# Attention scores of a multi-query kernel: the queries of two heads as one stationary operand of 64 rows and 128 columns

## The chip, the cores and the metric

The kernel runs on one core of one Trainium2 chip. The metric is the device time of one execution in microseconds (us); the smaller is the better. A core has five engines that run side by side, each through its own instructions in their order, and that wait for each other by semaphores: TensorE (PE, matrix products; its weight loads are listed apart as PEld), VectorE (DVE), ScalarE (ACT), GpSimd (POOL) and SyncE (SP), which issues most of the transfers.

## The reference

A multi-query attention with one null key, causal and masked, over 64 sequences of 128 tokens with 512 features, 16 heads of 64 and one head of keys and values; all in float32.

```python
xn = layernorm(x, g_in)
q = (xn @ Wq).reshape(b, n, H, DH).transpose(0, 2, 1, 3) * scale   # H = 16, DH = 64
kv = xn @ Wkv
k, v = kv[..., :DH], kv[..., DH:]
# null key and value put ahead of k and v; null bias ahead of attn_bias
sim = jnp.einsum('bhid,bjd->bhij', q, k) + bias
sim = where(causal, neg, sim); sim = where(mask, sim, neg)
attn = softmax(sim)
out = jnp.einsum('bhij,bjd->bhid', attn, v) ... @ Wo
return x + layernorm(out, g_out)
```

The change is in the product `einsum('bhid,bjd->bhij', q, k)`, the scores.

## The kernel before, in words

The 64 sequences are taken in groups of four (`g`, 16 groups) for the projections of queries, keys and values, and in pairs (`d`, 32 pairs) for the attention. The program is in one fixed order, written out by hand: after a start-up, which holds the scores of pair 0, it calls `turn(d)` and `body(d)` or `body_full(d)` for the pairs up to 29, then `turn_end` and `body_end` for the last two, then `body_last`. The order of the calls is the order of the instructions on each engine. `turn(d)` holds the scores of the pair's two sequences, `a` and `b`, and the value products of the pair before; `body_full(d)` holds the exponentials of the pair and fills TensorE meanwhile with the query products of the next group (lines 603 and 697), the key and value products (line 404) and the output products (line 998) of the pair before.

The queries of a group lie in the tiles `qT[g, j, h]`, 128 partitions each. The partitions are two heads (`r`) of 64 features each; along the free axis come `f % 2`, the sequence, the half `hf` of the sequence's 128 queries, the half `u` of the heads, and 64 queries. So one head is given by `u` (2), `f` (4) and `r` (2). The keys lie in `kT`, held twice: on the partitions 0 to 63 and, copied there, on 64 to 127, since both `r` need the same keys.

`scores(b, hf, tiles)` (line 765) makes the scores of one sequence for half of its queries. For `hf = 0` these are the first 64 queries, which by causality need 64 keys (`nk = 64`); for `hf = 1` the last 64, with all 128 keys. The result stands in PSUM, in one room for each `r`, with the partitions (`u`, query) and the free axis (`f`, key): two heads above each other. In the loops over `f`, `r` and `u`, each product on line 780 contracts over 64 partitions (the rows of head `r`), has 64 stationary columns (the queries of one head) and 64 or 128 moving columns (the keys), and it writes 64 partitions, 0 to 63 or 64 to 127 by `u`. There are 16 such products for each sequence and half, 2,048 in the program. The rooms go by the tags of their PSUM pools (`sc_Y`, `sc_w`, `sc_a`, `sc_X`, `sc_c`, and `ps` for the room of two banks); the rooms of `r = 0` and of `r = 1` are always apart.

`scores_add` (DVE, line 795) then adds the scores onto bias and mask in SBUF, `scores_max` (DVE, line 802) takes the row maxima, `exps` (ACT, line 811) the exponentials with their sums, `rinv` and `scale` (DVE 829, POOL 833) divide, `blocks_T` (DVE, line 849) transposes, and `values` (TensorE, line 911) multiplies by the values, in products of 32 rows and 64 columns.

In `turn(d)` the order on TensorE is: scores of `a` and of `b` for `hf = 0`, scores of `a` for `hf = 1`, scores of `b` for `hf = 1`, then the value products of the pair before. So a pair has one block of scores, between the output products (line 998, 128 rows and 128 columns) and the value products.

Of the kernel before, what the change touches and what calls it, by code (L numbers as in the profile page):

```python
# [17 lines left out]
def kernel(  # L18
# [59 lines left out]
    nc = tc.nc  # L78
    B, N, DIM = x.shape
    H = attn_bias.shape[0]  # L80
    DH = w_kv.shape[1] // 2
# [8 lines left out]
    Q = 32  # L90
# [182 lines left out]
    xT, qT, vr = {}, {}, {}  # L273
# [117 lines left out]
    kT = hp.tile([P, NQ, GB, Q], FP, tag="kT", name="kT", bufs=1)  # L391
# [365 lines left out]
    def rooms(b, hf, tiles):  # L757

        nk = N if hf == 1 else NL
        return [  # L760
            pool.tile([P, NF, nk], FP, tag=tag, name=f"sc_{b}_{hf}_{tag}")
            for pool, tag in tiles
        ]

    def scores(b, hf, tiles=None):
        g, t = divmod(b, GB)
        nk = N if hf == 1 else NL
        if tiles is None:
            whole = ps_s.tile([P, 2, NF * nk], FP, tag="s", name=f"ps_{b}_{hf}")
            whole = whole.rearrange("p r (f j) -> p r f j", f=NF)  # L770
            home = [whole[:, r] for r in range(2)]
            pss[b, hf] = whole
        else:
            home = rooms(b, hf, tiles)
            pss[b, hf] = home
        for f in range(NF):
            for r in range(2):
                rows = slice(r * DH, (r + 1) * DH)
                for u in range(2):
                    nc.tensor.matmul(  # L780
                        home[r][u * DH : (u + 1) * DH, f, :],
                        qT[g, f // 2, t // 2][rows, f % 2, t % 2, hf, u],
                        kT[rows, 0 : nk // Q, t, :],
                        start=True,
                        stop=True,
                    )

    pss = {}

# [302 lines left out]
    def turn(d):  # L1092

        a, b, p = 2 * d, 2 * d + 1, 2 * d - 2
        g = d // 2 + 1
        homes = (ps_y, "Y"), (ps_q, "a")
        if d == 1:
            homes = homes[::-1]
        scores(a, 0, (homes[0], (ps_w, "w")))
        scores(b, 0, (homes[1], (ps_w, "w")))  # L1100
        scores(a, 1)
        scores(b, 1, ((ps_y, "X"), (ps_q, "c")))
        scores_add(a, 0)
        scores_add(b, 0)
        scores_max(a, 0)
        scores_add(a, 1)
        scores_add(b, 1)
        po = values_rooms(p)
        steady = 3 < d < PAIRS - 2
        values(p, WIDE if steady else ())  # L1110
        values(p + 1, (WIDE if d % 2 else WIDE[1:]) if steady else ())
        if d % 2 and (d + 1) // 2 < NG:
            mask_neg((d + 1) // 2)
        bias_add(a + 2)
        if d % 2 == 0:
            token_sum(g, 1)
            token_sum(g, 2)
        exps(a, 0)
        values_out(p, po)
# [715 lines left out]
```

## Time and profile before

| what | value |
|---|---|
| median of 3 runs | 1023.64 us (1023.05 to 1023.94) |
| the profiled execution, its own time | 1022.45 us |
| its span, first to last instruction | 1020.6 us |
| granted TensorE clock, mean | 1.000 |
| busy: TensorE products, weight loads | 1012.9 us, 902.0 us |
| busy: VectorE, ScalarE, GpSimd | 860.8, 672.8, 775.0 us |
| records of products on line 780 | 4,096, as many of weight loads |

The profile is of one execution. Its span is 1.85 us shorter than the time that this execution was given, and that time 1.2 us shorter than the median. "Busy" counts the union of the records of an engine; the ends of products on TensorE are modelled, so a record's start is firmer than its length. A form such as `64*64 64x128 f32` is a product of 64 rows and 64 stationary columns, whose moving operand has 64 partitions and 128 columns. A row of the waits tells who waited for whom, the total in us, how often, and the longest.

### The profile page before, as it was taken

The numbers are of one execution on the slowest core, as the hardware profiler recorded it, in microseconds if no ns is written. First come the engines' busy times: TensorE is split into PE (matmuls) and PEld (weight loads), VectorE is DVE, ScalarE is ACT, GpSimd is POOL, SyncE is SP. The second block draws the span as 40 slices with busy tenths as digits, with TensorE's granted clock in tenths as the row PEclk, the third lists the DMA queues.
The fourth block names the chain that finished last, engine by engine and source line by source line (L and its number), as shares of the span: only waits on it lengthen the run. The fifth ranks groups of instructions, "written<-read, shape, count | busy, mean of one in ns | idle before, by whom it ended". The sixth has DMA issues, their size and how long they took to land.

```text
span 1020.6 us, 31143 instructions
## 1 busy us (share of the span) xinstructions
PE 1012.9 (99%) x12285; PEld 902.0 (88%) x12285; DVE 860.8 (84%) x1849; ACT 672.8 (66%) x2675; POOL 775.0 (76%) x621
## 2 busy tenths in 40 slices
PE   9999999999999999999999999999999999999997
PEld 9888888888888888888888888888888888888886
DVE  6877778888888988889888888888888888878787
ACT  5766677656677565686666776566765667856583
POOL 4997779678696876959768596785968769587686
PEclk9999999999999999999999999999999999999999
DMA  7415243151431425224152341514314152141221
GB/s 219 139 31 151 67 117 112 31 163 65 143 99 61 120 67 152 88 76 124 51 161 76 105 121 35 164 63 138 102 49 136 64 152 89 71 103 33 68 85 62
DMA packets 73833, 100.84 MB, mean 99 GB/s; under 512 B 32212, under 2 KB 36056, under 8 KB 71896
## 3 DMA queue, kind: packets, MB, share of 16 engines
q1 hardware_dynamic: 73392, 98.47, 32.3%
q8 instruction: 96, 1.57, 0.6%
q14 instruction: 49, 0.40, 0.1%
q10 hardware_dynamic: 296, 0.40, 0.1%
HBM read 63.19 MB, written 33.55 MB: 95 GB/s over the span
## 4 chain that ended last, share of the span: by engine, by line
PE 95%; ACT 2%; POOL 1%; DVE 1%; issue 0%; DMA 0%; POOLq 0%; DVEq 0%
PE pyX L998 20%; PE pa L603 13%; PE pi L697 11%; PE pyY L998 10%; PE po L911 8%; PE pkv L404 6%; PE pyw L998 5%; PE pc L603 4%; PE ps L780 3%; PE pq L499 3%; PE pa L554 2%; PE sc_X L780 2%; PE sc_Y L780 2%; PE pc L697 2%; ACT s L811 2%; PE pc L554 1%
## 5 line engine op out<-in xcount | busy, mean ns | idle before, releaser
L811 ACT ACTIVATE s<-s,nmax 128x65 f32<-128x65 f32 (+1 forms) x1024 | 370.9, 366 | 62.2 <-DVE nmax L802 62.2
L833 POOL TENSOR_TENSOR s<-s,rinv 128x512 f32<-128x512 f32 (+1 forms) x132 | 189.7, 1448 | 115.4 <-DVE rinv L829 112.9
L745 POOL TENSOR_TENSOR s<-biasp,mneg 128x1552 f32<-128x1552 f32 (+1 forms) x65 | 206.2, 3175 | 30.7 <-DVE s L795 21.2
L811 ACT ACTIVATION_READ_ACCUMULATOR s<-s,nmax 128x1 f32 x1024 | 194.5, 190 | 0.0
L725 DVE TENSOR_TENSOR qT<-pi,qT 128x128 f32<-128x128 f32 (+1 forms) x376 | 123.6, 340 | 35.9 <-PE pi L697 28.8
L1034 ACT COPY y<-pyX 128x256 f32<-128x256 f32 x29 | 10.8, 373 | 180.7 <-PE pyX L998 180.7
L802 DVE TENSOR_REDUCE nmax<-s 128x8 f32<-128x1032 f32 (+1 forms) x128 | 121.6, 950 | 0.1
L849 DVE STREAM_TRANSPOSE sb<-s 128x1536 f32<-128x1536 f32 (+1 forms) x68 | 113.6, 1674 | 2.1 <-POOL s L833 1.7
L998 PE MATMUL pyX<-wT,oT 128*128 128x256 f32 x464 | 109.7, 379 | 0.0
L998 PE MATMUL pyX<-wo,oT 128*128 128x256 f32 x464 | 109.7, 379 | 0.0
L978 POOL TENSOR_TENSOR oT<-oT 128x512 f32<-128x512 f32 x64 | 81.1, 1278 | 26.4 <-PE pyw L998 24.1
L998 PEld LDWEIGHTS pyX<-wT,oT 128*128 128x128 f32 x464 | 84.0, 190 | 9.2
L998 PEld LDWEIGHTS pyX<-wo,oT 128*128 128x128 f32 x464 | 84.0, 190 | 9.2
L911 PE MATMUL po<-sb,vr 32*64 32x128 f32 (+1 forms) x3700 | 86.2, 315 | 0.1
L911 PEld LDWEIGHTS po<-sb,vr 32*64 32x64 f32 x3700 | 74.8, 131 | 9.5 <-issue 5.3
L930 ACT ACTIVATE oT<-po,nv 128x512 f32<-128x512 f32 (+1 forms) x127 | 73.9, 660 | 0.4 <-PE po L911 0.4
L404 PE MATMUL pkv<-xT,wkv 128*128 128x256 f32 x256 | 63.3, 391 | 0.0
L998 PE MATMUL pyw<-wo,oT 128*128 128x256 f32 x256 | 60.5, 379 | 0.0
L998 PE MATMUL pyY<-wo,oT 128*128 128x256 f32 x256 | 60.5, 379 | 0.0
L998 PE MATMUL pyY<-wT,yS 128*128 128x256 f32 x256 | 60.5, 379 | 0.0
L614 ACT COPY qT<-pa 128x512 f32<-128x512 f32 x78 | 45.4, 582 | 17.7 <-PE pa L603 17.7
L404 PEld LDWEIGHTS pkv<-xT,wkv 128*128 128x128 f32 x256 | 46.2, 189 | 10.0 <-issue 4.8
(231 smaller groups left out, 2510.1 us busy)
## 6 DMA issues: line engine op xcount, KB each, us to landing
res<-in_x_dram SPq DMA_DIRECT2D x64, 256.0 KB
out_dram<-y SPq DMA_DIRECT2D x63, 256.0 KB
x<-in_x_dram SPq DMA_DIRECT2D x62, 256.0 KB
xd<-xb SPq DMA_DIRECT2D x14, 1024.0 KB
xT<-xd SPq DMA_DIRECT2D x56, 256.0 KB
vr<-vd SPq DMA_DIRECT2D x64, 128.0 KB
kT<-kT SPq DMA_DIRECT2D x32, 64.0 KB
vd<-vb SPq DMA_DIRECT2D x32, 64.0 KB
```

What stands on the lines that cost most here:

```text
L404: nc.tensor.matmul(pkv, wkv[:, kc, :], xT[g][:, t : t + 2, kc, :], start=(kc == 0), stop=(kc == KC - 1),)
L603: nc.tensor.matmul(prod[tag][:, i], w[:, kc, f * P : (f + 1) * P], t[:, :, kc, :], start=first, stop=(kc == HK - 1), skip_group_check=not ...
L697: nc.tensor.matmul(to, inner_w[k][i][:, h], inner_x[k, g][i], start=(i == 1), stop=True, skip_group_check=(i != 1),)
L725: nc.vector.tensor_tensor(o, p, o, ALU.add)
L745: nc.gpsimd.tensor_tensor(S[b][:, :, keys], biasp[:, :, keys], mneg[:, t, keys] .unsqueeze(1) .broadcast_to([P, R8, keys.stop - keys.start ...
L802: nc.vector.tensor_reduce(nmax[b][:, hf], S[b][:, :, WITH_NULL[hf]], AX.X, ALU.max, negate=True)
L811: nc.scalar.activation(row, row, AF.Exp, bias=nmax[b][:, hf, k : k + 1], accum_out=rsum[b][:, hf, k : k + 1],)
L833: nc.gpsimd.tensor_tensor(sv, sv, rinvs[b, hf][:, lo:hi].unsqueeze(2).broadcast_to([P, hi - lo, sv.shape[2]]), ALU.mult,)
L849: nc.vector.transpose(sbs[b][:, :, lo:hi].rearrange("p j e q -> p e j q"), S[b][:, lo:hi, 1 : ROW - 1].rearrange("p e (j k) -> p e j k", k=Q),
L911: nc.tensor.matmul(po[s][rows, to : to + n], vr[g][quad, t, PLACE[j], :], sb[quad, slots, r * NF : (r + 1) * NF, :], start=(turn == 0), st ...
L978: eng.tensor_tensor(o, a, b, op)
L998: nc.tensor.matmul(prod[key], h[:, c, :], w[:, c, :], start=(start and c == 0), stop=(c == HC - 1), skip_group_check=not start,)
```

## The change

The loop over `u` goes. One product takes the queries of both heads `u` as one stationary operand of 64 rows and 128 columns, which lie side by side in `qT`, and writes all 128 partitions of the room. Rows, moving operand, rooms, and the order of `f` and `r` are the same.

```diff
         for f in range(NF):
             for r in range(2):
                 rows = slice(r * DH, (r + 1) * DH)
-                for u in range(2):
-                    nc.tensor.matmul(
-                        home[r][u * DH : (u + 1) * DH, f, :],
-                        qT[g, f // 2, t // 2][rows, f % 2, t % 2, hf, u],
-                        kT[rows, 0 : nk // Q, t, :],
-                        start=True,
-                        stop=True,
-                    )
+                nc.tensor.matmul(
+                    home[r][:, f, :],
+                    qT[g, f // 2, t // 2][rows, f % 2, t % 2, hf].rearrange(
+                        "p u i -> p (u i)"
+                    ),
+                    kT[rows, 0 : nk // Q, t, :],
+                    start=True,
+                    stop=True,
+                )
```

On TensorE, in a pair's turn, this is the place where the scores of `b` with 64 keys end (`sc_0_a` and `sc_0_w`, the rooms of `r = 0` and `r = 1`) and those of `a` with 128 keys follow (`ps_1`, both rooms), then the first of `b` with 128 keys (`sc_1_X`, `sc_1_c`). Each row gives the size of the result and, where there are several alike, their number. Before:

```order
L780 MATMUL sc_0_a<-kT,qT_1_0_1693 64x64 x2
L780 MATMUL sc_0_w<-kT,qT_1_0_1693 64x64 x2
L780 MATMUL ps_1_1959<-kT,qT_0_0_1308 64x128 x8
L780 MATMUL ps_1_1959<-kT,qT_1_0_1693 64x128 x8
L780 MATMUL sc_1_X<-kT,qT_0_0_1308 64x128 x2
L780 MATMUL sc_1_c<-kT,qT_0_0_1308 64x128 x2
```

And of the changed kernel, at the same place, where the product stands on line 779:

```order
L779 MATMUL sc_0_a<-kT,qT_1_0_1565 128x64
L779 MATMUL sc_0_w<-kT,qT_1_0_1565 128x64
L779 MATMUL ps_1_1815<-kT,qT_0_0_1212 128x128 x4
L779 MATMUL ps_1_1815<-kT,qT_1_0_1565 128x128 x4
L779 MATMUL sc_1_X<-kT,qT_0_0_1212 128x128
L779 MATMUL sc_1_c<-kT,qT_0_0_1212 128x128
```

Two products of 64 result partitions became one of 128, everywhere alike; nothing else stands in another place, on TensorE or on the other engines.

## The prediction

> **What bounds the kernel now.** I read the page's first and fourth parts, then TensorE's waits, then the instructions of the changed line 780, then the timeline of one steady pair.
>
> ```profile
> PE 1012.9 (99%) x12285; PEld 902.0 (88%) x12285; DVE 860.8 (84%) x1849; ACT 672.8 (66%) x2675; POOL 775.0 (76%) x621
> ...
> PE 95%; ACT 2%; POOL 1%; DVE 1%; issue 0%; DMA 0%; POOLq 0%; DVEq 0%
> ```
>
> A matmul engine at 99% need not be the limit, since its ends are modelled. Its waits settle it. The whole list for TensorE has two rows, 2.0 us in all:
>
> ```profile
> PE busy L1667 <- POOL neg L255: 1.4, 1, 1.4
> PE pyc L998 <- DVE y L1032: 0.6, 1, 0.6
> ```
>
> So TensorE is never held up by another engine between the start and the last pair, and its instructions run in a fixed order. A nanosecond more in its stream is a nanosecond more of time, and one less is one less until an engine behind it becomes late. The scores are this much of that stream (columns: window, length, PE busy and records, weight-load busy and records, clock, DMA share, GB/s), and the forms of two of their tiles follow (min/median/max in ns):
>
> ```profile
> 0.00:1020.60 1020.60, 93.95 (x4096) 85.46 (x4096) 1.00 0.33 99
> ```
>
> ```profile
> L780 PEld LDWEIGHTS ps<-kT,qT x1056: 133/133/135, 29.7 to 982.1; 64*64 64x64 f32 x176
> L780 PE MATMUL ps<-kT,qT x1056: 269/269/272, 29.8 to 982.2; 64*64 64x128 f32 x176
> L780 PEld LDWEIGHTS sc_w<-kT,qT x1024: 129/135/135, 29.3 to 981.3; 64*64 64x64 f32 x171
> L780 PE MATMUL sc_w<-kT,qT x1024: 218/218/267, 29.3 to 981.3; 64*64 64x64 f32 x171
> ```
>
> The kernel issues 64 x 2 x 16 = 2,048 score products and the trace holds 4,096 records of them, so each f32 product is two records, each with its own weight load. Durations overlap and say nothing of the pace; starts do. The timeline of one pair (start, length to the end of the merged row, engine, line, tile, count):
>
> ```profile
> 526.17 1.24 PE L998 MATMUL pyX<-wT,oT 128*128 128x256 f32 x5
> 527.34 0.27 PE L780 MATMUL sc_Y<-kT,qT 64*64 64x64 f32 x2
> 527.36 0.27 PE L780 MATMUL sc_w<-kT,qT 64*64 64x64 f32 x2
> 527.45 0.23 PE L780 MATMUL sc_Y<-kT,qT 64*64 64x64 f32 x2
> 527.46 0.23 PE L780 MATMUL sc_w<-kT,qT 64*64 64x64 f32 x2
> 527.51 0.23 PE L780 MATMUL sc_Y<-kT,qT 64*64 64x64 f32 x2
> ...
> 528.32 1.06 PE L780 MATMUL ps<-kT,qT 64*64 64x128 f32 x32
> ...
> 529.96 0.28 PE L780 MATMUL sc_X<-kT,qT 64*64 64x128 f32 x2
> 529.98 0.28 PE L780 MATMUL sc_c<-kT,qT 64*64 64x128 f32 x2
> 530.18 2.63 PE L911 MATMUL po<-sb,vr 32*64 32x256 f32 x116
> ```
>
> Four records start within some 20 ns, one in each 64 x 64 quarter of the array (two r by two u), then the next four a fixed step later: four quarters work at once. With 64 keys there are 15 steps from 527.45 to 528.32, **58.0 ns each**; with 128 keys 15 steps from 528.32 to 529.96, **109.3 ns each**. Per sequence and half there are 4 f x 2 records = 8 steps, so a sequence costs 8 x 58.0 + 8 x 109.3 = **1338 ns**.
>
> **The change part by part.** *Fewer records.* A step now holds two records (r = 0 and 1) instead of four, each over 64 rows and 128 columns. This is no saving by itself: the quarters of one step already ran side by side, and the number of steps stays at 8 per half, because the array streams the keys past u = 0 and u = 1 at once before and after. Moving columns per step are the same.
>
> *A wider weight load.* Before, the 128 query columns of one step reached a row half as two loads of 64 running together; now as one load of 128. What that costs is read where a load is exposed, at the first product after a switch of shape. The form rows of the key and value products, 128 columns, show it:
>
> ```profile
> L404 PEld LDWEIGHTS pkv<-xT,wkv x256: 186/190/192, 15.0 to 937.8; 128*128 128x128 f32 x128
> L404 PE MATMUL pkv<-xT,wkv x256: 379/379/483, 15.1 to 938.1; 128*128 128x256 f32 x128
> ```
>
> The first record lasts 483 - 379 = 104 ns longer there, against 267 - 218 = 49 ns in the rows of sc_w with 64 columns. The load durations say the same, 190 against 133 to 135 ns. So 64 columns more cost about 55 ns of loading.
>
> Is that hidden behind the stream? A row with 128 loaded columns and 64 moving ones does not exist in this trace; the nearest has 128 and 128, the inner query products, between products of 256:
>
> ```profile
> 516.99 0.61 PE L697 MATMUL pi<-xI,wN 128*128 128x128 f32 x4
> 517.44 0.39 PE L697 MATMUL pi<-xI,wq 128*128 128x128 f32 x2
> 517.66 0.39 PE L697 MATMUL pi<-xT,wL 128*128 128x128 f32 x2
> 517.88 0.39 PE L697 MATMUL pi<-xS,wq 128*128 128x128 f32 x2
> 518.11 1.89 PE L998 MATMUL pyX<-wT,oT 128*128 128x256 f32 x8
> 519.84 0.38 PE L697 MATMUL pi<-xI,wS 128*128 128x128 f32 x2
> ...
> 520.95 0.38 PE L998 MATMUL pyX<-wo,oT 128*128 128x256 f32 x1
> ```
>
> Ten records from 516.99 to 518.11 and ten from 519.84 to 520.95 (two are shown of the second ten) take 2.23 us: **111.5 ns each**. The eight of 256 columns take 1.73 us, 216 ns each: there the load of 104 ns is hidden, so the array loads the next operand while it streams. But only one ahead: a step cannot be shorter than the load of the next step. With 64 keys the stream needs at most 58.0 ns and the load 104; the step becomes the load's. Bounds for it: 58.0 if the load is no limit after all; 104, the bare load; 111.5, the row with the same load; 58.0 + 55 = 113, if today's step is already the load's. I take 111.5, since that row has the very load and only the stream differs, which here is shorter. With 128 keys load and stream are level, as in that row: from 109.3 to 113, again 111.5.
>
> The sum: a sequence costs 16 x 111.5 = 1784 ns, 446 more; over 64 sequences **+28.5 us**: 8 x 53.5 x 64 = 27.4 us from the 64-key halves and 8 x 2.2 x 64 = 1.1 us from the 128-key halves.
>
> *Entering the scores.* The first step of a pair's scores exposes its load: 104 instead of 49 ns, 32 times, **+1.8 us** (none at the least). The idle gaps at the switches stay in number (weight-load rows, us in total, times, longest):
>
> ```profile
> PEld sc_Y L780 <- issue: 9.8, 31, 0.3
> PEld po L911 <- issue: 5.3, 31, 0.2
> ```
>
> They are 0.32 and 0.17 us. A switch to or from the new shape is not in the trace; either could take the other's value, 0.15 x 31 = 4.7 us up or down. I leave them.
>
> *Who hides it.* Nothing: TensorE has no wait to give up. DVE, ACT and POOL, behind it, get 0.9 us more per pair. Only at the end is the path elsewhere (chain of waits: start, us, what):
>
> ```profile
> 970.23 5.86 ACT s L811 x32
> ...
> 988.78 5.86 ACT s L811 x32
> ```
>
> There the scores still come first, but those of a pair's last half run beside these exponentials; at most four halves of 0.45 us, 1.8 us, may vanish. I take none off.
>
> Together +30.3 us: the profiled execution, 1022.45 us with a span of 1020.6, goes to 1052.8. The median of the runs is 1.2 us above it, so the forecast is 1023.64 + 30.3 = **1053.9 us**.
>
> **The rivals.** *Loads are no limit (faster).* If the array keeps its step at the stream and what fixed cost there is belongs to the instruction, halving the records helps. The stream's share of a step is 109.3 - 58.0 = 51.3 ns per 64 keys, which leaves a fixed 6.7 ns; half of it gone is 3.35 x 16 x 64 = 3.4 us, so 1020.2; nothing gone is 1023.6. It decides from the point where the load of 128 columns takes under 58 ns. For it: loads of 64 columns are wholly hidden today. Against it: 104 against 49 ns exposed.
> The Trainium skill, TensorEngine Tiling (Array Packing), section Instruction Overhead, puts a fixed 60 cycles on every matmul; an estimate from it, 25 ns for each of 2,048 records less over four quarters, would be 13 us saved. The 6.7 ns of the rows do not bear that out.
>
> *Load and stream of a row half take turns.* Then a step is 104 + 51 = 155 ns with 64 keys and 104 + 103 = 207 with 128: 8 x 362 = 2896 ns, 1558 more per sequence, +99.7 us, 1123 us. Against it: the 216 ns steps of 256 columns hide their load on the same rows.
> The Trainium skill, TensorE: Matmul & The Clock Gate, section The mechanism (Part 3), has loads overlap running matmuls only where the row group differs. By that rule this rival would hold; the trace does not agree with it, in the 216 ns.
>
> *The two row halves no longer run together.* Then every record has its own 111.5 ns: 32 x 111.5 - 1338 = 2230 ns, +142.7 us, 1166 us. For it: only the row split is left to make them independent. Against it: the value products on line 911 (32 rows by 64 columns) leave 116 records in 2.63 us, 23 ns each, where one of them alone has 128 or 256 moving columns, 109 ns or more; so at least five run at a time, more than the two column halves alone could hold, and row groups do run together.
>
> *The change is undone on the way*, each product being split again into 64 columns: 1023.6. Against it: the program's own order lists half the products with 128 rows of output.
>
> **How the numbers follow.** The forecast's mechanism gets 0.86, turns 0.03, no row halves together 0.04, loads no limit 0.05, undone 0.02. Within the forecast: low, 8 x (104 - 58.0) x 64 = 23.6 us less the 1.8 of the end, 1045.4; high, (16 x 113 - 1338) x 64 = 30.1, with 1.8 for entering and 4.7 for a dearer switch out, 1060.2. The range is 1045 to 1060; it holds nearly all of the 0.86 and none of the rest. About 0.2%, 2 us, is what a measurement can tell here. Slower: 0.86 + 0.03 + 0.04 = 0.93. Loads no limit spreads from no change to -3.4 us: 0.03 faster and 0.02 the same; with the undone case the same is 0.04.
>
> **What would show it.** Right: 2,048 records of the score line, with load durations near 190 ns; steps near 111 ns in both halves; a pair's scores from 2.84 us to about 3.8; pairs 0.95 us further apart; no new TensorE wait. Wrong: steps of 58 ns with 64 keys (loads no limit), steps over 150 ns (turns, or row halves apart), or the same steps and an unchanged span, in which case the slack I deny exists. If the steps are right and the total is not, the entry or the end was mis-sized.

## The result and the profile after

The changed kernel takes **1051.66 us** (median of 6 runs, 1051.22 to 1052.47) against 1023.16 us (median of 6, 1022.89 to 1023.94): a ratio of **1.0277** (95% interval 1.0264 to 1.0291), 28.5 us slower. Forecast were 1053.9 us, 30.3 us slower, in a range of 1045 to 1060. The profiled execution took 1051.69 us with a span of 1049.6 us; that of before 1022.45 and 1020.6.

The page of the changed kernel, first and fourth part:

```profile
PE 1041.7 (99%) x10237; PEld 933.3 (89%) x10237; DVE 865.1 (82%) x1849; ACT 677.1 (65%) x2675; POOL 774.0 (74%) x621
...
PE 95%; ACT 2%; POOL 1%; DVE 1%; issue 0%; DMA 0%; POOLq 0%; DVEq 0%
```

TensorE has 2,048 records fewer and is busy 28.8 us longer; the other engines kept their busy time within 5 us. Its waits are still next to nothing:

```profile
PE busy L1668 <- POOL neg L255: 1.4, 1, 1.4
PE pyc L999 <- DVE y L1033: 0.6, 1, 0.6
PE pa L554 <- issue: 0.2, 1, 0.2
```

The score products, now on line 779, as a window over the whole span (length, products busy and records, weight loads busy and records, clock, DMA share, GB/s), and two of their tiles by form (min/median/max in ns):

```profile
0.00:1049.60 1049.60, 123.75 (x2048) 117.04 (x2048) 1.00 0.32 96
```

```profile
L779 PEld LDWEIGHTS ps<-kT,qT x528: 188/188/188, 30.2 to 1011.6; 64*128 64x128 f32 x176
L779 PE MATMUL ps<-kT,qT x528: 272/272/325, 30.3 to 1011.7; 64*128 64x128 f32 x176
L779 PEld LDWEIGHTS sc_w<-kT,qT x512: 182/188/188, 29.3 to 1010.7; 64*128 64x128 f32 x171
L779 PE MATMUL sc_w<-kT,qT x512: 272/272/320, 29.3 to 1010.8; 64*128 64x64 f32 x171
```

Half the records, 29.8 us more of busy time. A load lasts 188 ns where it lasted 133 to 135. And the timeline of a steady pair gives the steps:

```profile
542.42 0.32 PE L779 MATMUL sc_Y<-kT,qT 64*128 64x64 f32 x1
542.43 0.32 PE L779 MATMUL sc_w<-kT,qT 64*128 64x64 f32 x1
542.58 0.27 PE L779 MATMUL sc_Y<-kT,qT 64*128 64x64 f32 x1
...
544.15 0.27 PE L779 MATMUL sc_a<-kT,qT 64*128 64x64 f32 x1
...
545.21 0.27 PE L779 MATMUL sc_X<-kT,qT 64*128 64x128 f32 x1
...
545.99 0.27 PE L779 MATMUL sc_X<-kT,qT 64*128 64x128 f32 x1
...
546.20 2.63 PE L912 MATMUL po<-sb,vr 32*64 32x256 f32 x116
```

Two records start together, 7 ns apart, one for each row half. With 64 keys there are 14 steps from 542.58 to 544.15, 112 ns each (58.0 before); with 128 keys 7 steps from 545.21 to 545.99, 111 ns each (109.3 before). In the trace's own nanoseconds the 14 steps take 1563 ns, **111.6** each; in the same unit the 15 steps before are 875 ns, 58.3 each. The whole block of a pair goes from 2.84 us to 546.20 - 542.42 = 3.78 us. One step per block looks longer, where the keys change from 64 to 128. The loads show why that is no delay:

```profile
544.09 0.19 PEld L779 LDWEIGHTS sc_a<-kT,qT 64*128 64x128 f32 x1
544.10 0.19 PEld L779 LDWEIGHTS sc_w<-kT,qT 64*128 64x128 f32 x1
544.20 0.98 PEld L779 LDWEIGHTS ps<-kT,qT 64*128 64x128 f32 x16
545.10 0.19 PEld L779 LDWEIGHTS sc_X<-kT,qT 64*128 64x128 f32 x1
```

The loads of `ps`, eight for each row half, begin 0.11 us after the last ones of `sc_a` and take 0.90 us to the next tile's, 112 ns each: the loads run on evenly, and only the recorded start of a product moves against them, by some 53 ns, when its stream gets longer.

### The profile page after: what moved, and what is told of

Read it like the earlier page. It is cut to its first block, busy times and chain, and to the rows that moved or that the text cites. A ratio compares the mean times of both kernels' runs of the same rounds, so it can differ in the third digit from the quotient of the medians.

```text
span 1049.6 us, 27047 instructions
## 1 busy us (share of the span) xinstructions
PE 1041.7 (99%) x10237; PEld 933.3 (89%) x10237; DVE 865.1 (82%) x1849; ACT 677.1 (65%) x2675; POOL 774.0 (74%) x621
## 4 chain that ended last, share of the span: by engine, by line
PE 95%; ACT 2%; POOL 1%; DVE 1%; issue 0%; DMA 0%; POOLq 0%; DVEq 0%
PE pyX L999 19%; PE pa L603 13%; PE pi L697 10%; PE pyY L999 10%; PE po L912 8%; PE pkv L404 6%; PE pyw L999 5%; PE pc L603 4%; PE sc_Y L779 3%; PE ps L779 3%; PE pq L499 3%; PE sc_a L779 2%; PE sc_X L779 2%; PE pa L554 2%; PE pc L697 2%; ACT s L812 2%
## 5 line engine op out<-in xcount | busy, mean ns | idle before, releaser
L979 POOL TENSOR_TENSOR oT<-oT 128x512 f32<-128x512 f32 x64 | 81.1, 1278 | 28.8 <-PE pyw L999 26.5
L779 PE MATMUL sc_w<-kT,qT 64*128 64x64 f32 x512 | 64.1, 275 | 0.0
L779 PEld LDWEIGHTS sc_w<-kT,qT 64*128 64x128 f32 x512 | 59.5, 188 | 0.0
```

The costliest lines, as they stand in the source:

```text
L779: nc.tensor.matmul(home[r][:, f, :], qT[g, f // 2, t // 2][rows, f % 2, t % 2, hf].rearrange("p u i -> p (u i)"), kT[rows, 0 : nk // Q, t, :],
```

## The experiments

The theory: a step of the scores lasts as long as the longer of its stream and the load of the next stationary operand; the load goes with the number of stationary columns; TensorE waits for nobody, so the total follows. The rivals: the wide shape costs time as such; load and stream take turns; the row halves share one path for their loads. Each kernel was timed beside the kernel before on the same chip.

**One half of the products alone.** The wide product where `hf == 1` (128 keys), the two narrow ones where `hf == 0`, and, in the second kernel, the other way round (`if hf == 0`):

```diff
+                if hf == 1:
+                    nc.tensor.matmul(
+                        home[r][:, f, :],
...
+                else:
+                    for u in range(2):
+                        nc.tensor.matmul(
+                            home[r][u * DH : (u + 1) * DH, f, :],
```

> The theory: a step of the scores lasts as long as the longer of two things, its stream of keys and the load of the next stationary operand, and TensorE, which waits for nobody, hands every nanosecond on. Here only the products with 128 keys have 128 stationary columns; those with 64 keys have 64 columns again. Theory: steps of 58 ns with 64 keys and 111.6 ns with 128 keys, so 1.1 us more than before, and one more switch of shape in each pair, about 92 ns of gap and 104 ns of exposed load, 33 times, 6.5 us: 1031 us. Rival, that the wide shape costs time as such in both halves alike: half of the 28.5 us stays, 14 us, and with the switches 1044 us.

> The other half alone: 128 stationary columns with 64 keys, 64 columns with 128 keys. Theory: steps of 111.6 ns with 64 keys and 109.3 ns with 128; 27.4 us more than before, 1.8 us for entering, and one more switch in each pair, 92 and 49 ns, 33 times, 4.7 us: 1057 us. Rival, that the wide shape costs alike in both halves: 14 us and the switches, 1042 us.

Measured: wide for 128 keys **1030.20 us**, ratio 1.007 (1.0055 to 1.0085) to 1022.96; wide for 64 keys **1055.49 us**, ratio 1.0317 (1.0302 to 1.0333). In the timeline of the kernel that is wide for 128 keys the switch of shape stands in the middle of a block:

```profile
532.11 0.23 PE L791 MATMUL sc_a<-kT,qT 64*64 64x64 f32 x2
532.12 0.22 PE L791 MATMUL sc_w<-kT,qT 64*64 64x64 f32 x2
532.28 1.16 PE L780 MATMUL ps<-kT,qT 64*128 64x128 f32 x16
533.27 0.27 PE L780 MATMUL sc_X<-kT,qT 64*128 64x128 f32 x1
```

From the last narrow step to the first wide one are about 0.17 us instead of 58 ns, and the eight steps of `ps` to the next tile take 0.99 us instead of 8 x 111.6 = 893 ns, the exposed load. Of the 7.2 us, 16 x 2.3 ns in each of 32 pairs, 1.2 us, belong to the steps with 128 keys. That switch, 0.11 and 0.10 us by these rows, makes up the rest: 33 of them are 6.9 us, of which some 0.9 us came back elsewhere. The loss is in the 64-key half. The rival of a cost in both halves alike (1044 and 1042 us) falls.

**The stream doubled.** In both kernels the products of the first 64 queries stream all 128 keys, into rooms of 128 keys of which 64 are read; the scores that are used are the same.

```diff
-        nk = N if hf == 1 else NL
+        nk = N
...
-                nc.vector.tensor_tensor(sv[:, r], pv[r], sv[:, r], ALU.add)
+                nc.vector.tensor_tensor(
+                    sv[:, r], pv[r][:, :, 0 : sv.shape[3]], sv[:, r], ALU.add
+                )
```

> The changed kernel, but the products of the first 64 queries stream all 128 keys too, into rooms of 128 keys of which 64 are read. Theory: the load of 128 columns lasts 111.6 ns anyway and a stream of 128 keys hides behind it, so doubling the stream of half of the products costs nothing: steps of 111.6 ns throughout and the changed kernel's 1051.7 us within 1 us. Rival, that load and stream add up or take turns in part: 51 ns more in 8 steps of each of 64 sequences, 26 us, 1078 us.

> The same doubling of the stream in the kernel before (64 stationary columns). Theory: here the stream sets the step, which goes from 58.0 to 109.3 ns in 8 steps of each of 64 sequences, 26.3 us: 1049.5 us, so that with and without the change the kernels come within about 4 us of each other. Rival, that something else than the load of 128 columns slows the wide shape: the 28 us between the two shapes stay, and this kernel is at 1049.5 while the one with the wide shape is at 1078, or this one stays near 1023 us if the step of 58 ns isn't the stream's.

Measured: with the change **1051.57 us** (1051.24 to 1051.77), without it **1048.31 us** (1048.20 to 1048.41), the kernel before 1022.96. The wide kernel with the stream doubled:

```profile
542.82 0.27 PE L779 MATMUL sc_Y<-kT,qT 64*128 64x128 f32 x1
...
544.39 0.27 PE L779 MATMUL sc_a<-kT,qT 64*128 64x128 f32 x1
...
544.50 1.06 PE L779 MATMUL ps<-kT,qT 64*128 64x128 f32 x16
545.39 0.27 PE L779 MATMUL sc_X<-kT,qT 64*128 64x128 f32 x1
```

14 steps from 542.82 to 544.39 are 112 ns, as with 64 keys. Twice the stream is free in the wide shape and costs 25.4 us in the narrow one. So load and stream do not add up or take turns, on the same rows either; the stream hides behind the load. What a product writes, twice as much here, does not set the step of the wide shape either. It is also the other view of the change: it threw away what the short stream of the 64-key half had saved.

**96 columns.** The wide product with 96 stationary columns; the last 32 queries of the heads with `u = 1` are left out.

```diff
-                    home[r][:, f, :],
+                    home[r][0:96, f, :],
...
-                    ),
+                    )[:, 0:96],
...
```

> The changed kernel with 96 stationary columns instead of 128: the last 32 queries of the heads with u = 1 are left out, and the addition of the scores leaves out their partitions. Shape, rows, records and moving columns are as in the changed kernel. Theory: the load goes with the columns, halfway between 49 and 104 ns, so a step with 64 keys lasts about 58 + 27 = 85 ns; with 128 keys the stream is the longer again, 109.3 ns: 216 ns more for each sequence than before, 13.8 us and 0.9 us for entering, 1038 us. Rival, that the shape of 64 rows by the full width costs its 111.6 ns whatever is loaded: 1051.7 us.

Measured **1036.22 us**, ratio 1.0123 (1.0106 to 1.0140) to 1023.28. The timeline, in the 64-key part:

```profile
535.24 0.24 PE L779 MATMUL sc_Y<-kT,qT 64*96 64x64 f32 x1
...
536.43 0.24 PE L779 MATMUL sc_a<-kT,qT 64*96 64x64 f32 x1
...
536.51 1.07 PE L779 MATMUL ps<-kT,qT 64*96 64x128 f32 x16
```

14 steps from 535.24 to 536.43: 85 ns. Rows, records and streams on TensorE are those of the changed kernel; only the columns differ, and the step goes with them. A cost of the shape as such falls.

**The row halves in turn.** The loops over `f` and `r` exchanged in the changed kernel.

```diff
-        for f in range(NF):
-            for r in range(2):
+        for r in range(2):
+            for f in range(NF):
```

> The changed kernel with the loops over f and r exchanged: four products on the rows 0 to 63, then four on the rows 64 to 127. Theory, that each row half needs 111.6 ns for its own load and that the two halves load side by side: if TensorE can't reach ahead past eight records, the halves no longer overlap, 32 steps of 111.6 ns for a sequence and 143 us over the kernel before, 1166 us; if it can, 1051.7 us stays. Rival, that the two row halves share one path for their loads and take turns of 56 ns on it, which also makes 111.6 ns: with one half at a time a step is 58 ns with 64 keys and 109 ns with 128, 16 of each, 85 us over the kernel before, 1109 us.

Measured **1083.49 us**, ratio 1.0588 (1.0566 to 1.0609): none of the three numbers. The timeline shows a mixture:

```profile
557.76 0.77 PE L779 MATMUL sc_Y<-kT,qT 64*128 64x64 f32 x5
558.26 0.32 PE L779 MATMUL sc_w<-kT,qT 64*128 64x64 f32 x1
558.37 0.27 PE L779 MATMUL sc_Y<-kT,qT 64*128 64x64 f32 x1
558.42 0.27 PE L779 MATMUL sc_w<-kT,qT 64*128 64x64 f32 x1
558.48 0.27 PE L779 MATMUL sc_Y<-kT,qT 64*128 64x64 f32 x1
...
562.51 2.63 PE L912 MATMUL po<-sb,vr 32*64 32x256 f32 x116
```

Five records of the first row half (`sc_Y`) start before the first of the other half (`sc_w`); from then on the last three of the first overlap with it. The kernel issues all eight records of `sc_Y` ahead of those of `sc_w`, so by these rows TensorE starts products out of their order. The five take 0.77 us; the first record alone, with its exposed load, lasts 0.32; so the four steps of the lone half are still (0.77 - 0.32) / 4 = 112 ns, and when both halves run each keeps 0.11 us. So a row half needs 111.6 ns for its own load with nobody beside it: the rival of one shared path, 58 ns alone, falls. The theory's two numbers were for no reaching ahead and for enough of it; TensorE reaches ahead by a part of a room's eight records. A pair's block takes 562.51 - 557.76 = 4.75 us instead of 3.78, which in 32 pairs is 31 of the 31.8 us that this order costs.

**Less stream, narrow.** The three steps that a load sets or may set, 58.3 ns for 64 columns, 85.0 for 96 and 111.6 for 128, lie on one line. So the step before the change could have been the load's already, and not the stream's, as was assumed for the doubled stream. In the kernel before, the products of the first 64 queries take 32 keys; the other 32 get no scores added.

```diff
-                        home[r][u * DH : (u + 1) * DH, f, :],
+                        home[r][u * DH : (u + 1) * DH, f, 0 : nk if hf else Q],
...
-                        kT[rows, 0 : nk // Q, t, :],
+                        kT[rows, 0 : nk // Q if hf else 1, t, :],
...
```

> The kernel before with half the stream: the products of the first 64 queries take 32 of their 64 keys, and the other 32 get no scores added. The steps measured so far with a load that is the longer, 111.6 ns for 128 columns and 85.0 for 96, lie on a line of 0.83 ns for each column and 5 ns; it gives 58.3 ns for 64 columns. Theory: so the step of 58 ns in the kernel before is already the load's, streaming fewer keys saves nothing, 58 ns stay and 1023 us within 1 us. Rival: the step of 58 ns is the stream's; then it goes to about 32 ns, and 26 ns in 8 steps of 64 sequences save 13 us, 1010 us.

Measured **1022.15 us**, ratio 0.9991 (0.9982 to 1.0). The timeline:

```profile
527.13 0.23 PE L780 MATMUL sc_Y<-kT,qT 64*64 64x32 f32 x2
...
528.00 1.08 PE L780 MATMUL ps<-kT,qT 64*64 64x128 f32 x32
```

15 steps in 0.87 us, 58 ns each: half the stream saves no step time. The number of records does not set this step: with 32 columns, in the next run, a step of eight takes 55 to 57 ns where here one of four takes 58. With 64 keys the stream is an estimated 109.3 - 53.3 = 56 ns, since 128 columns more, 256 against 128, made 216 - 109.3 = 107 ns in the kernel before, and that run shows it. So before the change, load and stream were level in the 64-key half; any column more had to cost.

**The opposite: 32 columns.** Four products of 64 rows and 32 columns in place of the two narrow ones, in both halves.

```diff
+                for c in range(4):
+                    u, i = divmod(c, 2)
+                    nc.tensor.matmul(
+                        home[r][c * Q : (c + 1) * Q, f, :],
...
+                        tile_position=(r * DH, c * Q),
```

> The opposite of the change: 64 rows and 32 stationary columns, four column quarters for each row half, so eight records in a step instead of four. Theory: the load of 32 columns, 32 ns, is no limit any more, the step with 64 keys is the stream's, 109.3 less 53.3, 56 ns, and 109.3 ns with 128 keys: 2.3 ns in 8 steps of 64 sequences, 1.2 us less, and 0.9 us less for the exposed first load: 1021 us. Rival: sixteen loads and products that start in one step, 7 ns apart for each pair as measured, take 8 x 7 = 56 ns or more by themselves and a few ns too many make it slower: 62 ns and more in the 64-key steps, 1025 us or more.

Measured **1120.50 us**, ratio 1.0956 (1.094 to 1.0971), far worse than either number. The timeline of a block's start, and two rows of TensorE's waits (us in total, times, longest):

```profile
544.83 0.23 PE L781 MATMUL sc_Y<-kT,qT 64*32 64x64 f32 x4
544.86 0.23 PE L781 MATMUL sc_w<-kT,qT 64*32 64x64 f32 x4
544.88 0.24 PE L781 MATMUL sc_Y<-kT,qT 64*32 64x64 f32 x4
544.91 0.24 PE L781 MATMUL sc_w<-kT,qT 64*32 64x64 f32 x4
544.94 0.24 PE L781 MATMUL sc_Y<-kT,qT 64*32 64x64 f32 x4
...
545.16 0.22 PE L781 MATMUL sc_Y<-kT,qT 64*32 64x64 f32 x1
```

```profile
PE po L915 <- issue: 36.4, 31, 1.7
PE ps L781 <- issue: 19.4, 26, 1.8
```

After the first step, which has the exposed load, two take 55 and 57 ns (544.83 to 544.94), as the theory says. Then the records no longer come eight at a time but one or two, and TensorE stands idle among the scores, 19.4 us in all, and among the value products behind them, 36.4 us, up to 1.8 us at once, while the profile shows nothing that it waits for. Added up from one product's start to the next over the two traces, the score blocks take 44 us more than before the change, the value products, which are unchanged, 46 us more, and all else 8 us. The block holds 256 records instead of 128; that their supply runs dry fits these numbers, but no run tested it.

## Why the prediction was right

**The bound.** TensorE's products wait for 2.2 us after the change as for 2.0 us before. Nothing gave the time back in the steady part: the first score products of two pairs that lie 28 pairs apart, and those of the last two pairs, before:

```profile
91.86 0.27 PE L780 MATMUL sc_Y<-kT,qT 64*64 64x64 f32 x2
...
962.04 0.27 PE L780 MATMUL sc_Y<-kT,qT 64*64 64x64 f32 x2
...
980.40 0.27 PE L780 MATMUL sc_Y<-kT,qT 64*64 64x64 f32 x2
```

and of the changed kernel:

```profile
94.10 0.32 PE L779 MATMUL sc_Y<-kT,qT 64*128 64x64 f32 x1
...
990.16 0.32 PE L779 MATMUL sc_Y<-kT,qT 64*128 64x64 f32 x1
...
1009.05 0.32 PE L779 MATMUL sc_Y<-kT,qT 64*128 64x64 f32 x1
```

28 pairs take 896.06 instead of 870.18 us, 0.92 us more for each; 0.95 were forecast.

**The step.** 111.5 ns were taken for both halves, from the inner query products; 111.6 were measured. The reason held too. The bound of 113 ns stood for the case that the step of 58 ns is already the load's; the run with 32 keys shows that this is the case, so the row that I took and this bound tell of the same thing.

**Entering.** Forecast were 55 ns a block; in 0.92 us for a pair, of which 2 x 446 ns are the steps, 30 to 40 ns are left. The exposed load itself is there, but in two places: the first record of `sc_w` lasts 320 - 272 = 48 ns longer than the others, and the one of `ps` where the keys change 325 - 272 = 53 ns, together 101 ns for the 104 of the forecast. Where the other 15 to 25 ns came back is not shown.

**The end** is the term that was mis-sized, and its reason was wrong too. I took nothing off for the last two pairs, with 1.8 us as the most, for scores beside ScalarE's exponentials. From the first of them to the second the changed kernel takes 18.89 us (18.36 before), from there to the end of the span 40.55 (40.20): 0.53 and 0.35 us more where two full blocks would be 1.9. One microsecond came back, and it did so on TensorE. The weight loads of the value products in the last pair's turn, before and after the change:

```profile
982.36 0.29 PEld L911 LDWEIGHTS po<-sb,vr 32*64 32x64 f32 x12 [0.17 <-issue]
983.11 2.16 PEld L911 LDWEIGHTS po<-sb,vr 32*64 32x64 f32 x116 [0.46 <-DVE s L795]
```

```profile
1011.93 2.28 PEld L912 LDWEIGHTS po<-sb,vr 32*64 32x64 f32 x128
```

Before, they stop for 0.46 us, and for 0.33 us in the turn of the pair ahead, until VectorE has added scores (line 795): here the value products write into a room that scores have just left. The longer score steps give VectorE that time, and the stop is gone, with the 0.17 us ahead of it. The prediction's "TensorE has no wait to give up" came from the waits of the products alone; those of the weight loads held this one. Added up from one product's start to the next, the scores take 29.8 us more, the value products 1.2 us less and all else 0.4 us more, together the 29.0 us of the span.

The start, up to the pair at 91.86 us, grew by 2.24 us; two of its blocks are those of pair 0, each of one sequence. Together 2.24 + 25.88 + 0.53 + 0.35 = 29.0 us of span, 29.2 us from one profiled execution to the other, against 30.3. The median grew by 28.5 us, since the profiled execution of before was 0.7 us below its median and that of the changed kernel was not.

**The rivals.** The gain of 3.4 us rested on a fixed part of a step that was said to belong to the instructions; the step of four records with 64 columns lies on the line of the steps of two records with 96 and 128, with the same 5 ns besides, so it does not. Turns of load and stream (1123 us) fell by the doubled stream, row halves apart (1166 us) by the records that start 7 ns apart.

## What to carry to other kernels

Fewer and wider products were no saving here, since the narrow ones already ran side by side in the array: two operands of 64 columns load at once, one of 128 takes nearly twice as long (58.3 against 111.6 ns a step). Compare, for each step, the stationary columns to be loaded with the moving columns that hide them; with the moving side the shorter, every column more lengthens the step. And look first whether TensorE waits, in the rows of its weight loads too: where it doesn't, every such nanosecond arrives in the total.

## What the runs showed of the hardware

Steps set by the load took 58.3, 85.0 and 111.6 ns for 64, 96 and 128 columns of float32: 0.83 ns a column and 5 ns besides. The Trainium skill, TensorE: Matmul & The Clock Gate, section LDWEIGHTS (loading the stationary operand), gives the column count over 1.2 in ns whatever the rows; the slope agrees. The same page of the Trainium skill, section The mechanism (Part 3), has in its list loads overlap running products only where the row group differs, while its text also lets a load into the background weight buffer go ahead; the doubled stream, free behind loads on the same rows at 112 ns a step, does not agree with the first.

Not expected was how far order counts among products that could run together: the same products with `r` outside cost 31.8 us more, since the first room of a block ran five of its eight records before the next room's first. Nor was the limit on the other side: 256 records of 32 columns in a block started in step for four steps and then came in ones and twos, with idle times of up to 1.8 us in TensorE that nothing in the profile explains.
